# Second attention: quotients in the layout of the value products, causal mask in VectorE's row maximum

## Chip, cores and metric

The kernel runs on one core of a Trainium2 chip (trn2). The metric is the time of the device in microseconds (us). Before the change the median of three runs is 2527.09 us (2526.11 to 2530.27).

## What is computed

A post-norm stack over 4 sequences of 1024 tokens with 256 channels, in float32: an attention of 16 heads with 16 channels (normalised and rotated queries and keys), a gated feed-forward layer, a second causal attention, and a routed layer of 12 experts. The change lies in the second attention, of which the reference says:

```python
scores = jnp.einsum('bhqd,bhkd->bhqk', q, k) * scale
scores = jnp.where(causal[None, None], scores, -jnp.inf)
...
scores = scores + head_scales[None, :, None, None] * geo
attn = jax.nn.softmax(scores, axis=-1)
out = jnp.einsum('bhqk,bkhd->bqhd', attn, v).reshape(B, T, C)
return out @ w_out
```

It has 8 heads of 32 channels. The kernel treats them as 2 groups of 4 heads, so that a group fills 128 partitions.

## The kernel before

**The order of the work.** Up to the experts the order of the instructions on each engine is written out by hand: generators yield one unit of attention at a time, and `weave` puts "pieces" of other layers between the units (a piece is a few matmuls with what empties their bank). A tile is filled and freed in the order in which the code asks for it. The scores, the maxima and most pieces share a ring of six PSUM banks (`ps_s`); the value products have one bank (`ps_av`), and one more bank (`ps_m`) takes the denominators of the second attention or the pieces of the first. A first attention (`first_units`, 64 units) and a second attention of another batch (`second_units`, 36 units) follow each other, four times each.

**The second attention of a batch** (`second_units`, L1103). In the first 12 units only `Maxima1.unit` of group 0 runs; a unit is one tile of 128 queries against up to 512 keys, for four heads. L931 makes the scores. On the diagonal (8 of the 12 units) four more matmuls (L940) add a mask to the last 128 columns: they multiply an identity by the mask in bfloat16, and the product is summed in the same bank. Then VectorE takes the negated row maximum of each head (L942). Next come 12 units in which `Attend1` of group 0 and `Maxima1` of group 1 alternate, and 12 units of `Attend1` of group 1 alone. `split` (L944) and `turn` (L955) bring the maxima into the layout of the keys. `Attend1.scores` (L969) makes the transposed scores, from which ScalarE forms exponentials (L989); GpSimd clears what is above the diagonal (L992). `Attend1.values` (L1004) sums the value products in one bank, and in the other the denominators, in a layout where the heads and channels are partitions and 512 queries are columns.

**The end of a query block** (two blocks in each group, so 4 in a batch, 16 in all). ScalarE copies the two banks out (L1025). Some units later `unload` (L1028) turns both copies on TensorE (8 transposes, L1033) into two banks of the ring; VectorE then takes 16 reciprocals per partition (L1036) and multiplies (L1037) into `oq1`, in which tokens are partitions. For the projection `out_project` turns that back: `turn` (L544, four transposes at L549 and a copy at L552) four times in a batch, and `project` (L554) four times. With the residual, `add_residual` (L515) does six VectorE operations for each piece.

**The end of batch 3.** After its last unit the rows are routed, and dispatched in two halves (`dispatch`, L708), with GpSimd sending them; only then do the experts start (L1388).

**The start.** `project_qk(0, 0, first=True)` squares the projections on GpSimd into `sq` (L229, one buffer, in which `sinT` was loaded), and VectorE sums them (L233); L249 is a reciprocal of 128 columns.

Of the kernel before, what the change touches and what calls it, by code (L numbers as in the profile page):

```python
# [19 lines left out]
P = 128  # L20
# [15 lines left out]
def postln_layers_kernel(ctx: ExitStack, tc: tile.TileContext, a: dict, out: bass.AP):  # L36
# [5 lines left out]

    ident = const.tile([P, P], F32, name="ident")
    make_identity(nc, ident)
    mask_h = const.tile([P, P], BF16, name="mask_h")
    nc.gpsimd.memset(mask_h, 0.0)
    nc.gpsimd.affine_select(
        out=mask_h, in_=mask_h, pattern=[[-1, P]], compare_op=ALU.is_ge, fill=NEG, base=0, channel_multiplier=1
    )
    neg_half = const.tile([P, 1], F32, name="neg_half")  # L50
    nc.gpsimd.memset(neg_half, -0.5)
    ident_h = const.tile([P, P], BF16, name="ident_h")
# [49 lines left out]
    with ExitStack() as main:  # L102
# [42 lines left out]
            nc.sync.dma_start(w0[:, c], a["w0qkv"][c * P : (c + 1) * P, :])  # L145
        cosT = fa.tile([P, TB, D0], F32, tag="tmp", bufs=1, name="cosT")
        nc.scalar.dma_start(cosT, a["cos"].rearrange("(t p) d -> p t d", p=P))
        sinT = fa.tile([P, TB, D0], F32, tag="sq", bufs=1, name="sinT")
        nc.scalar.dma_start(sinT, a["sin"].rearrange("(t p) d -> p t d", p=P))
        gam = act.tile([P, 2, D0], F32, tag="avs", bufs=2, name="gam")  # L150
        nc.scalar.dma_start(gam.rearrange("p s d -> p (s d)"), a["gamma"].partition_broadcast(P))
# [51 lines left out]
        def project_qk(b, pr, first=False):  # L203


            def piece(j, big):
# [19 lines left out]
                part = ss[:, 2 * j : 2 * j + 2].rearrange("p t s h -> p (t s h)")  # L226

                def squares():
                    sq = fa.tile([P, 512], F32, tag="sq", bufs=1, name=f"sq0_{b}_{pr}_{j}")  # L229
                    nc.gpsimd.tensor_tensor(sq, x, x, ALU.mult)  # L230

                    def sums():
                        nc.vector.tensor_reduce(part, sq.rearrange("p (h d) -> p h d", d=D0), AX.X, ALU.add)  # L233

                    return sums
# [135 lines left out]
        class Maxima:  # L371


            def __init__(self, b, g, engines):
# [7 lines left out]
                def rotate(s, u):  # L382
                    eng, to_tok = engines[s], (self.tok, tokk)[s]
                    ts = slice(4 * u, 4 * u + 4)
                    x = xr[:, ts, s, hs, :]
                    y = fa.tile(
                        [P, 4, 4, D0], F32, tag="tmp" if eng is nc.gpsimd else "sq", bufs=1, name=f"y0_{b}_{g}_{s}_{u}"
                    )
# [12 lines left out]
                    eng.tensor_tensor(to_tok[:, ts, :, 0:D0], y, over_heads(bt[s], ts), ALU.add)  # L401
                    yield
# [134 lines left out]
                open_rows.add(key)  # L537
                later(1, root)

        def out_project(b, oqs, w, name):  # L540

            oTs = {}

            def turn(h, c, big):  # L544
                if c == 0:
                    oTs[h] = act.tile([P, 2, 512], F32, tag="hT", bufs=1, name=f"oT{name}_{b}_{h}")
                pt = bank(f"pt{name}_{b}_{h}_{c}", big)
                for i in range(4):
                    nc.tensor.transpose(  # L549
                        pt[:, i * P : (i + 1) * P], oqs[b][:, 4 * h + i, c * P : (c + 1) * P], ident  # L550
                    )
                nc.scalar.copy(oTs[h][:, c, :], pt)  # L552

            def project(j, big):  # L554
                ps = bank(f"pp{name}_{b}_{j}", big)
                for i in range(2):
                    q = slice((2 * j + i) % 4 * P, ((2 * j + i) % 4 + 1) * P)
                    for c in range(2):
                        nc.tensor.matmul(  # L559
                            ps[:, i * 256 : (i + 1) * 256], oTs[j // 2][:, c, q], w[:, c, :], start=c == 0, stop=c == 1  # L560
                        )
                for i in range(2):
                    add_residual(b, 2 * j + i, ps[:, i * 256 : (i + 1) * 256], name)

            out = []
            for h in range(2):
                out += [lambda big, h=h, c=c: turn(h, c, big) for c in range(2)]
                out += [lambda big, j=j: project(j, big) for j in (2 * h, 2 * h + 1)]
            return out

        def turn_x(b, j, name, big):

# [342 lines left out]
        class Maxima1:  # L915
# [7 lines left out]
            def unit(self, i):  # L923
# [5 lines left out]
                for h in range(4):  # L929
                    r = slice(32 * h, 32 * h + 32)  # L930
                    nc.tensor.matmul(  # L931
                        scs[h][:, :n],
                        qT[r, t * P : (t + 1) * P],
                        kT[r, u * 512 : u * 512 + n],
                        start=True,
                        stop=not diag,
                    )
                if diag:
                    for h in range(4):
                        nc.tensor.matmul(scs[h][:, n - P : n], ident_h, mask_h, start=False, stop=True)  # L940
                for h in range(4):
                    nc.vector.tensor_reduce(self.part[:, t, u, h : h + 1], scs[h][:, :n], AX.X, ALU.max, negate=True)  # L942

            def split(self, u):  # L944

# [17 lines left out]
        class Attend1:  # L963


            def __init__(self, m, oq):
                self.m, self.oq, self.b, self.g, self.pes, self.avs = m, oq, m.b, m.g, {}, {}

            def scores(self, i):  # L969
                qb, kt = sc_units[i]  # L970
# [33 lines left out]
            def values(self, i):  # L1004
# [15 lines left out]
                            stop=kt == 4 * qb + 3,  # L1020
                        )
                if kt == 4 * qb + 3:
                    for k in range(2):
                        d = act.tile([P, 512], F32, tag="avs", bufs=2, name=f"avs1_{self.b}_{self.g}_{qb}_{k}")
                        nc.scalar.copy(d, self.av[k])  # L1025
                        self.avs[qb, k] = d

            def unload(self, qb):  # L1028
                pt = [ps_s.tile([P, 512], F32, tag="s", name=f"pto1_{self.b}_{self.g}_{qb}_{k}") for k in range(2)]
                for k in range(2):  # L1030
                    for t in range(4):
                        q = slice(t * P, (t + 1) * P)
                        nc.tensor.transpose(pt[k][:, q], self.avs[qb, k][:, q], ident)  # L1033
                p4 = [t.rearrange("p (t h d) -> p t h d", t=4, h=4) for t in pt]
                rc = act.tile([P, 4, 4], F32, tag="rc", bufs=2, name=f"rc1_{self.b}_{self.g}_{qb}")
                nc.vector.reciprocal(rc, p4[1][:, :, :, 0])  # L1036
                nc.vector.tensor_tensor(  # L1037
                    self.oq[:, 4 * qb : 4 * qb + 4, P * self.g : P * self.g + P].rearrange(
                        "p t (h d) -> p t h d", h=4
                    ),  # L1040
                    p4[0],
                    rc.unsqueeze(3).to_broadcast([P, 4, 4, D1]),
                    ALU.mult,
                )


        groups = {}
        oq0, oq1, ends = {}, {}, {}
        both_pool = (nc.gpsimd, nc.gpsimd)

        def first_units(b):
# [50 lines left out]

        def second_units(b):  # L1103

            oq1[b] = act.tile([P, TB, C], F32, tag="oq", bufs=2, name=f"oq1_{b}")
            now = Maxima1(b, 0)
            for i in range(12):
                now.unit(i)
# [7 lines left out]
            last = None  # L1116
            for g in range(G1):
                nxt = Maxima1(b, g + 1) if g + 1 < G1 else None
                at = Attend1(now, oq1[b])
                for i in range(12):  # L1120
                    at.scores(i)
                    if i > 0:
# [2 lines left out]
                        last.values(11)  # L1125
                    if i == 1:
                        now.turn(1)
                        if last is not None:
                            last.unload(1)
# [8 lines left out]
                    if i == 6:  # L1138
                        at.unload(0)
                    yield  # L1140
                last, now = at, nxt
            last.values(11)
            last.unload(1)

        def weave(units, n, pieces, big, mid=(), at=0, side=(), side_at=0, rate=1):

# [132 lines left out]


        def first_end(b):
            return [lambda big: ends[b](big)] + out_project(b, oq0, w0p, "a0")

        def second_end(b):
            return out_project(b, oq1, w1o, "a1") + route(b)

        cut = 19
        stash = []
# [48 lines left out]
        nc.sync.dma_start(b2.rearrange("p e c -> p (e c)"), a["b2"].partition_broadcast(P))  # L1337
        weave(second_units(2), 36, first_end(3) + ffn0(3), True)
        out2 = second_end(2)
        straight(out2[:8] + project1(3))  # L1340
        out3 = out_project(3, oq1, w1o, "a1")
        st, tu, lo = route(3, True)
        steps2, sums2 = dispatch(2, True)
        weave(second_units(3), 23, out2[8:], True, out3[:4] + st[:2], 30, steps2, 18)
        flush()
        ordered.close()

        for piece in tu[:2] + out3[4:6] + lo[:2] + out3[6:]:
            piece(True)
            tick()  # L1350
        steps, sums = dispatch(3, True, 0)
# [186 lines left out]
```

## Time and profile before

| What | Value |
|---|---|
| median of three runs | 2527.09 us |
| the profiled execution, its own time | 2529.43 us |
| its span, first to last instruction | 2527.6 us |
| busy: TensorE, VectorE, ScalarE, GpSimd | 2364.4, 1364.7, 1024.8, 729.4 us |
| granted TensorE clock, mean | 0.956 |
| first 12 units of a second attention, batch 0 | 757.5 to 793 us from the start of the span |

The profile is of one execution. A group of instructions has a line of the code, an engine, an operation, what it writes and reads, a count, its busy time and the mean duration in ns of one. A float32 matmul shows as two records, a transpose or a bfloat16 matmul as one. The durations of matmuls overlap, so what a run of them costs TensorE is read from the distance between two starts in the timeline. "Idle before" is the time in which the engine had nothing to do before those instructions, with whom it waited for.

### The profile page before, as it was taken

Reading aid. Unit: us, or ns where it says so; the run is one execution under the profiler, and the core shown is the slowest. Engines: PE = TensorE matmul, PEld = TensorE weight load, DVE = VectorE, ACT = ScalarE, POOL = GpSimd, SP = SyncE. Lnnn points to the kernel's source line nnn. Section 1 sums busy time; section 2 is a strip of 40 time slices with the busy share of each in tenths; the row PEclk is TensorE's granted clock in tenths of the full one; section 3 lists DMA queues with packets and bytes.
Section 4 is the critical chain, followed back from the end, with each engine's and each line's share of the span. In section 5 each row is a group of like instructions: output and inputs, shape, how many; then the busy total and the mean of one; then the engine's idle time right before and its main releaser. Section 6 shows DMA issues by size and latency. Waiting matters only on the chain.

```text
span 2527.6 us, 36682 instructions
## 1 busy us (share of the span) xinstructions
PE 2364.4 (94%) x14452; PEld 1194.9 (47%) x14452; DVE 1364.7 (54%) x3157; ACT 1024.8 (41%) x2015; POOL 729.4 (29%) x1015
## 2 busy tenths in 40 slices
PE   6999999999999999999999999999999983999993
PEld 3343334444445543444445434445566442666662
DVE  6765654766657447787563677817435654111112
ACT  1355554545552445545424455461331331111122
POOL 5633623425114122454121320211110143122213
PEclk8999999999998999999989999999998985999996
DMA  3034212000000000001000000112000012444434
GB/s 92 29 119 135 84 59 83 1 27 1 1 1 27 1 1 1 23 26 51 31 1 1 1 1 1 48 33 86 1 1 1 1 51 68 108 111 103 117 72 141
DMA packets 79612, 109.89 MB, mean 43 GB/s; under 512 B 8784, under 2 KB 68432, under 8 KB 77776
## 3 DMA queue, kind: packets, MB, share of 16 engines
q1 hardware_dynamic: 54336, 80.48, 9.8%
q0 software_dynamic: 9984, 14.82, 3.0%
q10 hardware_dynamic: 15120, 12.27, 1.7%
q8 instruction: 113, 1.85, 0.3%
q14 instruction: 59, 0.48, 0.1%
HBM read 68.64 MB, written 38.90 MB: 43 GB/s over the span
## 4 chain that ended last, share of the span: by engine, by line
PE 85%; DVE 8%; DMA 3%; POOL 2%; ACT 1%; issue 1%; SPq 0%; ACTq 0%; DVEq 0%; POOLq 0%
PE sc L458 19%; PE av L476 10%; PE ph L1410 7%; PE py L1426 7%; PE gu L595 7%; PE mx L434 4%; PE sc L978 4%; PE mx L931 4%; PE p L898 4%; PE dn L611 3%; PE av L1015 3%; PE dn L1015 2%; DVE part L942 2%; PE qk L298 2%; PE ppa L559 2%; PE pt L425 2%
## 5 line engine op out<-in xcount | busy, mean ns | idle before, releaser
L437 DVE TENSOR_REDUCE part<-mx 128x1 f32<-128x512 f32 x1024 | 656.5, 685 | 344.3 <-PE mx L434 338.6
L467 ACT ACTIVATE pe<-sc 128x512 f32<-128x512 f32 x1024 | 554.1, 596 | 394.5 <-PE mx L434 341.8
L434 PE MATMUL mx<-kT,qT 32*128 32x512 f32 x2048 | 650.3, 644 | 6.0 <-DVE part L437 5.7
L458 PE MATMUL sc<-qT,kT 32*128 32x512 f32 x2048 | 616.3, 638 | 0.2 <-ACT pe L467 0.2
L458 PEld LDWEIGHTS sc<-qT,kT 32*128 32x128 f32 x2048 | 182.1, 183 | 223.8 <-issue 177.7
L476 PE MATMUL av<-pe,va 128*32 128x512 f32 x2048 | 272.8, 605 | 0.0
L942 DVE TENSOR_REDUCE part<-mx 128x1 f32<-128x512 f32 (+3 forms) x384 | 186.9, 550 | 152.3 <-PE mx L940 108.6
L434 PEld LDWEIGHTS mx<-kT,qT 32*128 32x128 f32 x2048 | 196.6, 185 | 52.7 <-DVE part L437 27.4
L989 ACT ACTIVATE pe<-sc 128x512 f32<-128x512 f32 (+3 forms) x384 | 157.6, 499 | 156.4 <-PE sc L978 156.1
L1410 PE MATMUL ph<-dmT,f 128*128 128x512 f32 x384 | 170.3, 602 | 4.4 <-DVE dmT L90 3.5
L1426 PE MATMUL py<-f,hTm 128*128 128x256 f32 x768 | 167.7, 379 | 0.0
L1418 ACT ACTIVATE hTm<-ph,b 128x512 f32<-128x512 f32 x96 | 60.8, 684 | 261.3 <-PE ph L1410 261.3
L992 POOL TENSOR_SCALAR_AFFINE_SELECT pe<-pe 128x256 f32<-128x256 f32 x128 | 51.7, 411 | 374.6 <-ACT pe L989 372.4
L1426 PEld LDWEIGHTS py<-f,hTm 128*128 128x128 f32 x768 | 145.9, 190 | 25.0 <-issue 5.7
L1430 POOL DMA_INDIRECT acc_d<-yo,dm x48 | 74.5, 1552 | 284.9 <-DVE yo L1428 238.8
L931 PE MATMUL mx<-kT,qT 32*128 32x512 f32 (+3 forms) x768 | 138.6, 593 | 8.5 <-DVE part L942 4.8
L356 POOL TENSOR_TENSOR ss<-ss,neg_half 128x16 f32<-128x16 f32 x48 | 138.7, 2907 | 0.5
L1427 DVE TENSOR_TENSOR yo<-py,b 128x256 f32<-128x256 f32 x48 | 20.4, 425 | 207.6 <-PE py L1426 207.6
L476 PEld LDWEIGHTS av<-pe,va 128*32 128x32 f32 x2048 | 40.3, 108 | 193.9 <-issue 183.9
L978 PE MATMUL sc<-qT,kT 32*128 32x512 f32 (+3 forms) x768 | 117.9, 546 | 1.7 <-DVE part L942 0.6
L1410 PEld LDWEIGHTS ph<-dmT,f 128*128 128x128 f32 x384 | 72.9, 192 | 94.9 <-issue 86.7
L595 PE MATMUL gu<-xTf,wg 128*128 128x256 f32 x384 | 107.7, 403 | 0.0
(357 smaller groups left out, 2938.0 us busy)
## 6 DMA issues: line engine op xcount, KB each, us to landing
f<-in_fc SPq DMA_DIRECT2D x14, 1024.0 KB, 5.0
f<-in_fc ACTq DMA_DIRECT2D x10, 1024.0 KB, 6.0
xink<-in_xT SPq DMA_DIRECT2D x32, 256.0 KB, 2.8
disp_d<-empty SPq DMA_DIRECT2D x12, 520.0 KB, 5.1
qk_d<-xs SPq DMA_DIRECT2D x6, 1024.0 KB, 3.9
xr<-qk_d SPq DMA_DIRECT2D x6, 1024.0 KB, 6.5
dm<-disp_d SPq DMA_DIRECT2D x11, 520.0 KB, 3.7
xinv<-in_xT SPq DMA_DIRECT2D x16, 256.0 KB, 3.1
```

The lines of the kernel that those rows point to most:

```text
L434: nc.tensor.matmul(sc, self.qT[r, t * P : (t + 1) * P], self.kT[r, u * 512 : (u + 1) * 512], start=True, stop=True)
L437: return lambda: nc.vector.tensor_reduce(self.part[:, t, u, h : h + 1], sc, AX.X, ALU.max, negate=True)
L458: nc.tensor.matmul(sc, self.m.kT[r, kt * P : (kt + 1) * P], self.m.qT[r, qb * 512 : (qb + 1) * 512], start=True, stop=True)
L467: nc.scalar.activation(self.pes[i, h // 2][:, h % 2, :], sc, AF.Exp)
L476: nc.tensor.matmul(self.av[32 * h : 32 * h + 32, :], va0[:, kt, 4 * self.g + h, :], self.pes[i, h // 2][:, h % 2, :], start=kt == 0, stop= ...
L595: nc.tensor.matmul(ps[:, i * 256 : (i + 1) * 256], w[:, c, f * P : (f + 1) * P], xT[j][:, c, :], start=c == 0, stop=c == 1,)
L931: nc.tensor.matmul(scs[h][:, :n], qT[r, t * P : (t + 1) * P], kT[r, u * 512 : u * 512 + n], start=True, stop=not diag,)
L942: nc.vector.tensor_reduce(self.part[:, t, u, h : h + 1], scs[h][:, :n], AX.X, ALU.max, negate=True)
L978: nc.tensor.matmul(scs[h][:, off:], ones_h[r, :] if w else kT[r, kt * P : (kt + 1) * P], (self.m.nmT if w else qT)[r, q], start=w == 0, st ...
L989: nc.scalar.activation(pe[:, j, off:], scs[2 * hp + j][:, off:], AF.Exp)
L1410: nc.tensor.matmul(ph[:, i * CAP : (i + 1) * CAP], f1[:, c, (f + i) * P : (f + i + 1) * P], dmT[:, c, :], start=c == 0, stop=c == 1,)
L1426: nc.tensor.matmul(py[:, :C], hT[:, f, c * P : (c + 1) * P], f2[:, f, :], start=f == 0, stop=f == FF1 // P - 1)
```

## The change

- At the end of a query block VectorE takes the reciprocal of the whole bank of denominators (128 x 512) and multiplies it with the bank of value products, in their own layout. The two copies, the eight transposes and `unload` are gone.
- The product is already what the projection needs as its weights, so the second attention's projection has no turns. Its list of pieces is 4 long and not 8, and the slices of these lists are changed to match. Two empty pieces (`wait`) stand behind the two projections in the last `weave`.
- On the diagonal, L940 is gone. VectorE adds a mask of 512 columns (zeros, and the triangle in the last 128) and takes the minimum of the negated sum in one instruction. It writes its sum into `masked`, of which there is one buffer.
- `sinT`, the squares at the start and one temporary go into a buffer ring of two (`q1`) and not into `sq`, which is gone.

```diff
+    mask_w = const.tile([P, 512], BF16, name="mask_w")
+    masked = const.tile([P, 512], BF16, name="masked")
...
-        sinT = fa.tile([P, TB, D0], F32, tag="sq", bufs=1, name="sinT")
+        sinT = act.tile([P, TB, D0], F32, tag="q1", bufs=G1, name="sinT")
...
-                    sq = fa.tile([P, 512], F32, tag="sq", bufs=1, name=f"sq0_{b}_{pr}_{j}")
+                    sq = act.tile([P, 512], F32, tag="q1", bufs=G1, name=f"sq0_{b}_{pr}_{j}")
...
+        def out_project1(b):
+            def project(j, big):
+                project_out(b, j, lambda c, i: oT1[b][:, c, (2 * j + i) * P : (2 * j + i + 1) * P], w1o, "a1", big)
+            return [lambda big, j=j: project(j, big) for j in range(4)]
...
-                        stop=not diag,
+                        stop=True,
                     )
-                if diag:
-                    for h in range(4):
-                        nc.tensor.matmul(scs[h][:, n - P : n], ident_h, mask_h, start=False, stop=True)
                 for h in range(4):
-                    nc.vector.tensor_reduce(self.part[:, t, u, h : h + 1], scs[h][:, :n], AX.X, ALU.max, negate=True)
+                    part = self.part[:, t, u, h : h + 1]
+                    if diag:
+                        nc.vector.tensor_tensor_reduce(
+                            masked[:, :n], scs[h][:, :n], mask_w[:, 512 - n :], -1.0, -NEG, ALU.add, ALU.min, part
+                        )
+                    else:
+                        nc.vector.tensor_reduce(part, scs[h][:, :n], AX.X, ALU.max, negate=True)
...
                 if kt == 4 * qb + 3:
-                    for k in range(2):
-                        d = act.tile([P, 512], F32, tag="avs", bufs=2, name=f"avs1_{self.b}_{self.g}_{qb}_{k}")
-                        nc.scalar.copy(d, self.av[k])
-                        self.avs[qb, k] = d
+                    rc = act.tile([P, 512], F32, tag="avs", bufs=2, name=f"rc1_{self.b}_{self.g}_{qb}")
+                    nc.vector.reciprocal(rc, self.av[1])
+                    nc.vector.tensor_tensor(
+                        self.oT[:, self.g, qb * 512 : (qb + 1) * 512], self.av[0], rc, ALU.mult
+                    )
...
-        straight(out2[:8] + project1(3))
-        out3 = out_project(3, oq1, w1o, "a1")
+        straight(out2[:4] + project1(3))
+        out3 = out_project1(3)
...
-        weave(second_units(3), 23, out2[8:], True, out3[:4] + st[:2], 30, steps2, 18)
+        weave(second_units(3), 23, out2[4:], True, out3[:2] + [wait] * 2 + st[:2], 30, steps2, 18)
...
-        for piece in tu[:2] + out3[4:6] + lo[:2] + out3[6:]:
+        for piece in tu[:2] + lo[:1] + out3[2:3] + lo[1:2] + out3[3:]:
```

More of the change, by code (lines that the diff above doesn't have):

```diff
@@ L44, in postln_layers_kernel @@
     make_identity(nc, ident)
-    mask_h = const.tile([P, P], BF16, name="mask_h")
-    nc.gpsimd.memset(mask_h, 0.0)
+    mask_w = const.tile([P, 512], BF16, name="mask_w")
+    nc.gpsimd.memset(mask_w, 0.0)
     nc.gpsimd.affine_select(
-        out=mask_h, in_=mask_h, pattern=[[-1, P]], compare_op=ALU.is_ge, fill=NEG, base=0, channel_multiplier=1
+        out=mask_w[:, 384:512],
+        in_=mask_w[:, 384:512],
+        pattern=[[-1, P]],
+        compare_op=ALU.is_ge,
+        fill=NEG,
+        base=0,
+        channel_multiplier=1,
     )
+    masked = const.tile([P, 512], BF16, name="masked")
     neg_half = const.tile([P, 1], F32, name="neg_half")
@@ L385, in rotate @@
                     x = xr[:, ts, s, hs, :]
-                    y = fa.tile(
-                        [P, 4, 4, D0], F32, tag="tmp" if eng is nc.gpsimd else "sq", bufs=1, name=f"y0_{b}_{g}_{s}_{u}"
-                    )
+                    if eng is nc.gpsimd:
+                        y = fa.tile([P, 4, 4, D0], F32, tag="tmp", bufs=1, name=f"y0_{b}_{g}_{s}_{u}")
+                    else:
+                        y = act.tile([P, 4, 4, D0], F32, tag="q1", bufs=G1, name=f"y0_{b}_{g}_{s}_{u}")
                     z = fa.tile([P, 4, 4, D0], F32, tag="tmpz", bufs=1, name=f"z0_{b}_{g}_{s}_{u}")
@@ L538, in add_residual, with project_out, out_project0 @@
                 later(1, root)
-        def out_project(b, oqs, w, name):
+        def project_out(b, j, oT, w, name, big):
+            ps = bank(f"pp{name}_{b}_{j}", big)
+            for i in range(2):
+                for c in range(2):
+                    nc.tensor.matmul(
+                        ps[:, i * 256 : (i + 1) * 256], oT(c, i), w[:, c, :], start=c == 0, stop=c == 1
+                    )
+            for i in range(2):
+                add_residual(b, 2 * j + i, ps[:, i * 256 : (i + 1) * 256], name)
+        def out_project0(b):
             oTs = {}
@@ L545, in turn @@
                 if c == 0:
-                    oTs[h] = act.tile([P, 2, 512], F32, tag="hT", bufs=1, name=f"oT{name}_{b}_{h}")
-                pt = bank(f"pt{name}_{b}_{h}_{c}", big)
+                    oTs[h] = act.tile([P, 2, 512], F32, tag="hT", bufs=1, name=f"oTa0_{b}_{h}")
+                pt = bank(f"pta0_{b}_{h}_{c}", big)
                 for i in range(4):
                     nc.tensor.transpose(
-                        pt[:, i * P : (i + 1) * P], oqs[b][:, 4 * h + i, c * P : (c + 1) * P], ident
+                        pt[:, i * P : (i + 1) * P], oq0[b][:, 4 * h + i, c * P : (c + 1) * P], ident
                     )
@@ L554, in project, with oT @@
             def project(j, big):
[L555 to L563, printed above, removed]
+                def oT(c, i):
+                    t = (2 * j + i) % 4
+                    return oTs[j // 2][:, c, t * P : (t + 1) * P]
+                project_out(b, j, oT, w0p, "a0", big)
             out = []
@@ L935, in unit @@
                         start=True,
-                        stop=not diag,
+                        stop=True,
                     )
-                if diag:
-                    for h in range(4):
-                        nc.tensor.matmul(scs[h][:, n - P : n], ident_h, mask_h, start=False, stop=True)
                 for h in range(4):
-                    nc.vector.tensor_reduce(self.part[:, t, u, h : h + 1], scs[h][:, :n], AX.X, ALU.max, negate=True)
+                    part = self.part[:, t, u, h : h + 1]
[3 more added lines that the diff above has]
+                        )
+                    else:
+                        nc.vector.tensor_reduce(part, scs[h][:, :n], AX.X, ALU.max, negate=True)
             def split(self, u):
@@ L963, in postln_layers_kernel, with __init__ @@
         class Attend1:
-            def __init__(self, m, oq):
-                self.m, self.oq, self.b, self.g, self.pes, self.avs = m, oq, m.b, m.g, {}, {}
+            def __init__(self, m, oT):
+                self.m, self.oT, self.b, self.g, self.pes = m, oT, m.b, m.g, {}
             def scores(self, i):
@@ L1022, in values @@
                 if kt == 4 * qb + 3:
-                    for k in range(2):
-                        d = act.tile([P, 512], F32, tag="avs", bufs=2, name=f"avs1_{self.b}_{self.g}_{qb}_{k}")
-                        nc.scalar.copy(d, self.av[k])
-                        self.avs[qb, k] = d
[L1028 to L1044, printed above, removed]
+                    rc = act.tile([P, 512], F32, tag="avs", bufs=2, name=f"rc1_{self.b}_{self.g}_{qb}")
+                    nc.vector.reciprocal(rc, self.av[1])
+                    nc.vector.tensor_tensor(
+                        self.oT[:, self.g, qb * 512 : (qb + 1) * 512], self.av[0], rc, ALU.mult
+                    )
         groups = {}
-        oq0, oq1, ends = {}, {}, {}
+        oq0, oT1, ends = {}, {}, {}
         both_pool = (nc.gpsimd, nc.gpsimd)
@@ L1103, in second_units @@
         def second_units(b):
-            oq1[b] = act.tile([P, TB, C], F32, tag="oq", bufs=2, name=f"oq1_{b}")
+            oT1[b] = act.tile([P, G1, S], F32, tag="oq", bufs=2, name=f"oT1_{b}")
             now = Maxima1(b, 0)
@@ L1118, in second_units @@
                 nxt = Maxima1(b, g + 1) if g + 1 < G1 else None
-                at = Attend1(now, oq1[b])
+                at = Attend1(now, oT1[b])
                 for i in range(12):
@@ L1127, in second_units @@
                         now.turn(1)
-                        if last is not None:
-                            last.unload(1)
                     if nxt is not None:
@@ L1137, in second_units @@
                             nxt.split(1)
-                    if i == 6:
-                        at.unload(0)
                     yield
@@ L1142, in second_units @@
             last.values(11)
-            last.unload(1)
         def weave(units, n, pieces, big, mid=(), at=0, side=(), side_at=0, rate=1):
@@ L1281, in first_end @@
         def first_end(b):
-            return [lambda big: ends[b](big)] + out_project(b, oq0, w0p, "a0")
+            return [lambda big: ends[b](big)] + out_project0(b)
         def second_end(b):
-            return out_project(b, oq1, w1o, "a1") + route(b)
+            return out_project1(b) + route(b)
         cut = 19
```

## The prediction

> **What bounds the kernel now.** I read the page, the chain that ended last, the groups by shape, the busy time by stages, and the timeline around one end of a query block.
>
> ```profile
> PE 85%; DVE 8%; DMA 3%; POOL 2%; ACT 1%; issue 1%; SPq 0%; ACTq 0%; DVEq 0%; POOLq 0%
> ```
>
> TensorE carries 85% of the chain, so a matmul that goes is worth its slot, and work added to VectorE is free where VectorE isn't late. Where is it late? The groups, then the first 12 units of each of the four second attentions:
>
> ```profile
> L942 DVE TENSOR_REDUCE part<-mx 128x1 f32<-128x512 f32 x192 | 119.2, 683 | 53.9 <-PE mx L931 43.4 <-PE mx L940 10.4
> ...
> L1037 DVE TENSOR_TENSOR oq<-pto,rc 128x512 f32<-128x512 f32 x16 | 11.1, 692 | 0.6
> ...
> L1036 DVE RECIPROCAL rc<-pto 128x16 f32<-128x16 f32 x16 | 4.1, 255 | 16.5 <-PE pto L1033 16.5
> ...
> L249 DVE RECIPROCAL ss<-ss 128x128 f32<-128x128 f32 x1 | 1.0, 953 | 0.4 <-ACT ss L248 0.4
> ```
>
> ```profile
> core 0: us, PE busy (x) PEld busy (x) DVE busy (x) ACT busy (x) POOL busy (x), PEclk, DMA share, GB/s
> 757.50:793.00 35.50, 33.93 (x182) 18.62 (x183) 27.74 (x67) 5.20 (x9) 16.78 (x10) 0.86 0.15 47
> 1240.50:1277.00 36.50, 35.08 (x172) 19.72 (x170) 25.95 (x62) 5.48 (x10) 14.73 (x8) 0.77 0.16 53
> 1703.00:1744.00 41.00, 38.48 (x217) 24.91 (x216) 37.63 (x98) 4.48 (x10) 3.73 (x8) 0.96 0.42 149
> 1926.00:1955.00 29.00, 27.38 (x124) 17.06 (x122) 25.27 (x64) 1.27 (x3) 1.86 (x4) 0.70 0.00 1
> ```
>
> VectorE is busy 71 to 92% of these (116.6 of 142 us), and TensorE's weight loads wait for its row maxima in the six-bank ring: VectorE sets the pace there. Once scores and values run too, it doesn't: in the window 829 to 841 VectorE is busy 6.36 of 12 us, TensorE all 12.
>
> ```profile
> 827.95 1.14 PE L931 MATMUL mx<-kT,qT 32*128 32x512 f32 x8
> 829.02 1.09 PE L1033 MATMUL pto<-ident,avs 128*128 128x128 f32 x8
> 829.95 1.03 PE L595 MATMUL gu<-xTf,wg 128*128 128x256 f32 x4
> ```
>
> ```profile
> 815.97 0.39 DVE L520 TENSOR_TENSOR x<-ppa,x 128x256 f32<-128x256 f32 x1
> ...
> 816.96 2.50 DVE L942 TENSOR_REDUCE part<-mx 128x1 f32<-128x512 f32 x4
> 819.38 0.73 DVE L100 TENSOR_SCALAR x<-x,mv_a,rs_a 128x256 f32<-128x256 f32 x2
> ```
>
> The eight turns of an unload take 0.93 us of TensorE (829.02 to 829.95). The second fence is VectorE at the end of a query block (batch 0, whose value products end at 815.3): a residual's six operations, then at once four maxima, then more. There it is late already.
>
> **What goes from TensorE.**
> - Turns of the quotients: 16 unloads at 0.93 us. Four stand at the end of a second attention and are counted with the stalls below; 12 × 0.93 = 11.2 us.
> - Turns before the projection: four transposes take 0.53 us (802.20 to 802.73). 16 pieces; three batches count, batch 3's with its end: 12 × 0.53 = 6.4 us.
> - Mask matmuls: four take 0.23 us (806.50 to 806.73). 64 diagonal units; in the 32 of the first stages VectorE paces, so 32 × 0.23 = 7.4 us.
> - The start: the squares alternate with their sums in one buffer (GpSimd's second square waits 4.49 us for the first sum, at 18.35). With two buffers I replay them from the arrivals of the projections (12.05, 14.28, 16.72, 19.08 us): the last sum ends at 21.2, not 23.9. All after it follows: 2.7 us.
>
> Sum 27.7 us. ScalarE's 48 copies of 0.6 us were off the path: nothing. SP and GpSimd issue the same instructions as before.
>
> **What comes to VectorE: the reciprocal.** It grows from 16 to 512 columns. From 16 (255 ns) and 128 (953 ns) a column costs 6.23 ns, so 953 + 384 × 6.23 = 3345 ns (bounds: 3.2 to 3.6, with PSUM as source, as in the 16-column row). With the product (692 ns) VectorE is blocked for 4.05 us, 16 times, where ScalarE had copied in about 1.2 us. Queued behind it are the next unit's maxima, which free ring banks, and a piece's residual; waiting for it are TensorE's next values, since both accumulator banks are single.
> - Block 0 of group 0: four maxima stand behind it. In batches 0 and 1 the residual stands ahead, so all 4.05 us fall on the maxima (816.96 becomes 821.0), and the scores at 818.07 need banks that these free; with the diagonal's longer maxima before it 4.9 us each. In batch 2 a gate piece (1.9 us) covers part: 2.3. In batch 3 2.8. Sum 14.9.
> - Block 1 of group 0: no maxima, but the next values wait. Batch 0: VectorE ends `split` at 861.7, so quotients at 865.75, and the values that start at 863.10 wait 2.65. Batch 1 the same, batch 2 1.5, batch 3 2.1. Sum 8.9.
> - Block 0 of group 1: a piece and the scores lie between (3.2 us), so 1.1, 1.1, 0.1; in batch 3 there is no piece, and some 3.6 us of dispatch stand ahead of it on VectorE: 6. Sum 8.3.
> - Block 1 of group 1: before, TensorE waited 0.5 us for the copies and turned for 0.93; after, the first attention's maxima wait instead: 0.6 worse twice. In batch 3 the last pieces no longer wait for turns and copies, and GpSimd's sends set the pace anyway: I give back 4 us. Sum -2.8.
>
> Together 29.3 us (bounds: 15, if pieces hide more, and 40).
>
> **What comes to VectorE: the mask.** No row shows this instruction. Nearest is the product of 512 columns with a PSUM source, 692 ns, against 620 from start to start of the maxima (2.48/4). In the changed program's order three of four wait for VectorE's own last instruction, since `masked` is one buffer; the overlap of 65 ns goes. The Trainium skill (VectorE: DVE Perf Modes, section "Two Vector instructions with no wait between them") says that an operation that writes out an accumulator is two instructions, the second a read of it, which no row here shows. By the row alone one costs 0.10 us more than a maximum; by the rule, with a read of 0.075 us (start to start of the smallest operations at 2030.4) to 0.165 (their duration), 0.15 to 0.27. The changed order has these 256 reads; I take 0.22, 56 us of VectorE in all.
> - First stages: 32 units × 4 × 0.22 = 28 us to VectorE's 116.6, makes 145 of 142 us. Some 8 us of its gaps stay (it must wait for the first scores): 10 us longer. Bounds: by the row alone 13 us, which fits the gaps, so 0; at 0.27 and all gaps kept, 23.
> - Other diagonal units: the maximum starts 0.2 us earlier, TensorE's piece hides the rest, except behind a short piece: 3 us (0 to 8).
>
> **The clock.** The Trainium skill (TensorE: Matmul & The Clock Gate, "Why this matters for your kernels") wants no idle gap over some 3 us, else TensorE falls to half clock. The trace is stricter: from 769 to 781 the granted clock was 0.57, with no wait above 1.24 us. Half clock for some 3.4 us (the page's window) loses 1.7 us. By the rule three stalls (4.9, 4.9 and 6 us) qualify, 5.1 us; by the row all eight of 2 us and more might, 14 us. The 6 us one stands at batch 3's end, where GpSimd's sends set the pace, so I take two of the three, 3.5.
>
> **Sum.** -27.7 + 29.3 + 10 + 3 + 3.5 = +18 us on the profiled execution's 2529.4 us (2527.6 of span, 1.8 around it): 2547.5. That execution lay 2.3 us above the median of the runs, so 2545 us.
>
> **The rivals.** About 0.2% (5 us) is what a measurement can tell from no change.
> - VectorE pays more than TensorE gains: the forecast, 2532 to 2570. Against it: VectorE is only 54% busy over all. Chance 0.62.
> - TensorE's slots decide: the pieces between hide the reciprocal (15 us of stalls), the masked maximum fits the gaps (0), and the clock holds: -27.7 + 15 + 1 = -12, 2515 us. For it: 85% of the chain is TensorE. It decides once the fused maximum costs under 0.1 us extra and the stalls average below 1.5 us. Chance 0.14.
> - The two cancel, with a stall of some 1.5 us and 3 us in the first stages: 2522 to 2532. Chance 0.12.
> - The masked maximum streams slower than one column per 1.3 ns, or its read waits the pipeline out: 0.5 us extra gives 64 us to the first stages and drags the mixed units too: 2590. Against it: both two-input rows run at 1.3 to 1.6 ns a column. Chance 0.12.
>
> Faster 0.14, same 0.12, slower 0.74. The range for 8 in 10 is 2518 to 2578: the low end takes in most of the second rival, the high end the upper bounds of two terms together.
>
> **What would show it.** Right: reciprocals near 3.3 us; TensorE waiting for VectorE 2 to 5 us behind them; masked maxima of 0.7 us and reads of 0.1 to 0.2; first stages longer by 2 to 4 us each; mixed units away from block ends shorter by 0.2. Wrong: a reciprocal far from 3.3 us, a fused maximum that costs no more than the old one, or batch 3's end moving by more than a few us, which I know least.

## The result and the profile after

The changed kernel takes 2589.98 us, median of 4 runs (2588.65 to 2594.44); before, 2526.6 (2524.49 to 2530.27). The ratio is 1.0255 (95% interval 1.0239 to 1.0270): slower by 2.55%, outside the predicted range of 2518 to 2578. The profiled execution took 2590.03 us, with a span of 2588.3, 60.7 us more than before.

The chain of waits of the changed kernel:

```profile
PE 82%; DVE 11%; DMA 2%; POOL 2%; issue 1%; ACT 1%; SPq 0%; ACTq 0%; DVEq 0%; POOLq 0%
```

TensorE's share fell from 85 to 82%, VectorE's rose from 8 to 11%. The groups by shape give the new instructions' durations (busy us and mean ns after the bar, then the idle time ahead and what ended it):

```profile
L969 DVE TENSOR_REDUCE part<-mx 128x1 f32<-128x512 f32 x128 | 79.3, 682 | 34.3 <-PE mx L955 34.3
...
L1052 DVE RECIPROCAL rc<-dn 128x512 f32<-128x512 f32 x16 | 53.6, 3347 | 10.5 <-PE dn L1042 10.5
...
L965 DVE CUSTOM_DVE_ANT_0 masked<-mx,mask_w 128x512 bf16<-128x512 f32 x64 | 44.2, 690 | 14.3 <-PE mx L955 6.6 <-DVE part L965 0.5
...
L965 DVE DVE_READ_ACCUMULATOR2_ANT part<- 128x1 f32 x256 | 21.2, 83 | 0.0
```

The reciprocal takes 3347 ns (forecast 3345), the masked maximum 690 with a read of 83. So the single prices were right, and the sum was not. Where are the 60.7 us? Batch 0's four stages, before and after (first maxima, units with maxima, units without, next first attention; PEld is TensorE's loading of weights, PEclk the granted clock):

```profile
core 0: us, PE busy (x) PEld busy (x) DVE busy (x) ACT busy (x) POOL busy (x), PEclk, DMA share, GB/s
758.70:797.50 38.80, 37.09 (x204) 20.91 (x200) 32.01 (x82) 6.74 (x13) 18.63 (x13) 0.87 0.13 43
797.50:857.60 60.10, 60.03 (x498) 28.80 (x498) 32.44 (x77) 21.98 (x54) 15.00 (x21) 0.97 0.01 2
857.60:915.40 57.80, 57.29 (x484) 31.52 (x480) 15.32 (x40) 25.00 (x61) 7.31 (x18) 1.00 0.00 1
915.40:1243.10 327.70, 323.97 (x2032) 138.68 (x2032) 235.05 (x498) 176.63 (x335) 115.20 (x171) 0.99 0.06 20
```

```profile
754.40:797.90 43.50, 41.96 (x168) 25.05 (x164) 34.53 (x118) 6.85 (x13) 19.11 (x13) 0.66 0.13 38
797.90:861.70 63.80, 61.74 (x466) 27.94 (x465) 37.17 (x101) 20.89 (x52) 14.47 (x21) 0.96 0.01 1
861.70:923.90 62.20, 58.29 (x468) 30.50 (x466) 21.64 (x44) 23.19 (x56) 7.35 (x18) 0.97 0.00 1
923.90:1254.20 330.30, 326.23 (x2006) 137.23 (x2006) 239.64 (x498) 173.86 (x329) 115.20 (x171) 0.99 0.06 20
```

Each stage is longer, although TensorE has fewer instructions (466 for 498 in the second), and in three of four the clock is lower. In the second stage TensorE is busy 61.74 us for 60.03: less work, more time. The same cuts through all batches (profiled executions, us; the first maxima end where the first value product starts):

| part of the span | before | after | change |
|---|---|---|---|
| start, to the first maxima of second attention | 758.7 | 754.4 | -4.3 |
| first maxima, 4 batches | 171.7 | 187.1 | +15.4 |
| units of both groups, 4 batches | 467.1 | 503.3 | +36.3 |
| between the second attentions | 664.9 | 677.7 | +12.8 |
| after the last value product | 465.2 | 465.8 | +0.6 |

For the third and fourth row together (1132.0 us before, 1181.1 after) I split TensorE's time in three. The clock records have two values only, full and half. *Idle* is length minus busy time; *clock loss* is half of the busy time within half-clock stretches (an estimate: it takes a matmul to last twice as long there); the rest is *work*.

| us | before | after | change | forecast |
|---|---|---|---|---|
| idle | 18.3 | 46.4 | +28.1 | +32.3 (29.3 and 3) |
| clock loss | 7.9 | 31.4 | +23.5 | +3.5 |
| work | 1105.9 | 1103.2 | -2.7 | -25.0 (11.2, 6.4 and 7.4) |

The idle time came out about as forecast. The clock's loss is nearly seven times the forecast, and of the gain in work only a tenth is there. The timeline at the first block end of batch 0 shows both; first before the change, then after (idle time ahead in brackets; sc are scores, av value products, dn denominators):

```profile
818.07 1.54 PE L978 MATMUL sc<-qT,kT 32*128 32x512 f32 x7
...
820.18 1.06 PE L1015 MATMUL av<-pe,va 128*32 128x512 f32 x8
```

```profile
813.34 1.18 PE L1005 MATMUL sc<-qT,kT 32*128 32x512 f32 x8
...
817.22 3.34 DVE L1052 RECIPROCAL rc<-dn 128x512 f32<-128x512 f32 x1
...
818.33 1.86 PE L1005 MATMUL sc<-qT,kT 32*128 32x512 f32 x4
...
820.60 0.69 DVE L1053 TENSOR_TENSOR oT<-av,rc 128x512 f32<-128x512 f32 x1
821.20 2.48 DVE L969 TENSOR_REDUCE part<-mx 128x1 f32<-128x512 f32 x4
...
821.94 1.29 PE L1005 MATMUL sc<-qT,kT 32*128 32x512 f32 x3 [1.74 <-DVE part L969]
...
824.28 1.94 PE L1042 MATMUL av<-pe,va 128*32 128x512 f32 x8
...
825.98 1.39 PE L1042 MATMUL dn<-pe,ones 128*32 128x512 f32 x8
```

The scores wait for the maxima behind the quotient, as forecast. From the first score to the first value product it takes 5.95 us, before 2.11: 3.84 more. Only 1.74 of it counts as idle. Two heads' scores (4 records) start alone, one after the other, and are busy for 1.86 us, where the eight of four heads together take 1.18 (813.34); so a part of the stop hides in busy time. And the wait of 1.74 us is followed by a half-clock stretch from 823.3 to 826.7, and the eight value products in it take 1.94 us; eight of the same at full clock take 1.06 (at 837.35). At the second block end the single accumulator banks show as forecast, with 2.82 us for 2.65:

```profile
869.61 0.69 DVE L1053 TENSOR_TENSOR oT<-av,rc 128x512 f32<-128x512 f32 x1
...
870.45 1.39 PE L1042 MATMUL av<-pe,va 128*32 128x512 f32 x8 [2.82 <-DVE oT L1053]
```

Half clock follows here too (871.1 to 874.5), and at 929.1 after a wait of 1.29 us. It doesn't follow every stop: the same place in batch 2 has a wait of 2.43 us and full clock behind it.

```profile
1865.12 1.06 PE L1042 MATMUL av<-pe,va 128*32 128x512 f32 x8 [2.43 <-DVE oT L1053]
```

Of the 16 block ends of the changed kernel, 10 are followed by 3.4 or 6.8 us of half clock.

### The profile page after: what moved, and what is told of

Its sections match the earlier page's. It is cut to its first block, busy times and chain, and to the rows that moved or that the text cites. A ratio compares the mean times of both kernels' runs of the same rounds, so it can differ in the third digit from the quotient of the medians.

```text
span 2588.3 us, 36180 instructions
## 1 busy us (share of the span) xinstructions
PE 2393.7 (92%) x14004; PEld 1191.5 (46%) x14004; DVE 1435.3 (55%) x3413; ACT 1001.3 (39%) x1967; POOL 730.7 (28%) x1015
## 4 chain that ended last, share of the span: by engine, by line
PE 82%; DVE 11%; DMA 2%; POOL 2%; issue 1%; ACT 1%; SPq 0%; ACTq 0%; DVEq 0%; POOLq 0%
PE sc L467 18%; PE av L485 9%; PE ph L1416 7%; PE py L1432 6%; PE gu L619 6%; PE mx L443 5%; PE sc L1005 4%; PE mx L955 4%; PE p L922 3%; PE dn L635 3%; PE av L1042 3%; PE dn L1042 2%; PE ppa L554 2%; PE qk L306 2%; DVE rc L1052 2%; DVE masked L965 2%
## 5 line engine op out<-in xcount | busy, mean ns | idle before, releaser
L443 PE MATMUL mx<-kT,qT 32*128 32x512 f32 x2048 | 661.6, 644 | 8.2 <-DVE part L446 7.8
L467 PE MATMUL sc<-qT,kT 32*128 32x512 f32 x2048 | 624.5, 639 | 1.5 <-DVE part L446 1.1
L443 PEld LDWEIGHTS mx<-kT,qT 32*128 32x128 f32 x2048 | 200.0, 185 | 64.0 <-DVE part L446 34.8
L965 DVE CUSTOM_DVE_ANT_0 masked<-mx,mask_w 128x128 bf16<-128x128 f32 (+3 forms) x256 | 125.5, 490 | 127.3 <-PE mx L955 97.6
L955 PE MATMUL mx<-kT,qT 32*128 32x512 f32 (+3 forms) x768 | 156.7, 643 | 9.3 <-DVE part L969 3.5
L1424 ACT ACTIVATE hTm<-ph,b 128x512 f32<-128x512 f32 x96 | 60.7, 683 | 261.2 <-PE ph L1416 261.2
L1005 PE MATMUL sc<-qT,kT 32*128 32x512 f32 (+3 forms) x768 | 139.0, 563 | 7.5 <-DVE part L969 5.2
L955 PEld LDWEIGHTS mx<-kT,qT 32*128 32x128 f32 x768 | 77.1, 218 | 74.7 <-issue 29.8
```

Of the source, the lines that this page charges most:

```text
L443: nc.tensor.matmul(sc, self.qT[r, t * P : (t + 1) * P], self.kT[r, u * 512 : (u + 1) * 512], start=True, stop=True)
L467: nc.tensor.matmul(sc, self.m.kT[r, kt * P : (kt + 1) * P], self.m.qT[r, qb * 512 : (qb + 1) * 512], start=True, stop=True)
L955: nc.tensor.matmul(scs[h][:, :n], qT[r, t * P : (t + 1) * P], kT[r, u * 512 : u * 512 + n], start=True, stop=True,)
L965: nc.vector.tensor_tensor_reduce(masked[:, :n], scs[h][:, :n], mask_w[:, 512 - n :], -1.0, -NEG, ALU.add, ALU.min, part)
L1005: nc.tensor.matmul(scs[h][:, off:], ones_h[r, :] if w else kT[r, kt * P : (kt + 1) * P], (self.m.nmT if w else qT)[r, q], start=w == 0, st ...
```

## The experiments

Theory: the quotients' block ends cost most, by waits and by the half clock that follows them. Rival: the masked maxima cost most. The runs say how much each makes. Medians are us; each ratio is to the kernel before on the same chip, with its 95% interval.

**1. The start alone.** The kernel before with

```
-        sinT = fa.tile([P, TB, D0], F32, tag="sq", bufs=1, name="sinT")
+        sinT = act.tile([P, TB, D0], F32, tag="q1", bufs=G1, name="sinT")
```

and the same for `sq` and for VectorE's `y`.

> The kernel before with the third part of the change alone: sinT, the squares of the start and y of VectorE in the two-buffer ring q1. Forecast: 2.7 us less (2524). The stage table of the changed kernel's trace says 4.3 us less by the second attention of batch 0 (2522 to 2523), and nothing after that. Rival: the gain belongs to the rest of the change and this alone gives 0 to 1 us.

2521.58 (ratio 0.9986, 0.9977 to 0.9995; before 2525.51). The start gives 4 us. It is the reference for the next two.

**2. The quotients alone** (with the ring q1): the mask matmuls and plain maxima are put back in the changed kernel for diagonal units.

```
+                if diag:
+                    for h in range(4):
+                        nc.tensor.matmul(scs[h][:, n - P : n], ident_h, mask_h, start=False, stop=True)
...
-                        nc.vector.tensor_tensor_reduce(
-                            masked[:, :n], scs[h][:, :n], mask_w[:, 512 - n :], -1.0, -NEG, ALU.add, ALU.min, part
-                        )
```

> The changed kernel with the mask put back on TensorE (mask matmuls and plain maxima), so: new quotients, projection without turns, ring q1. My own terms: -11.2 - 6.4 - 4.3 (start as measured) + 29.3 + 3.5 (clock) = +11, so 2538 us. Theory 'quotients': the block ends cost more than I gave them, because the maxima behind the reciprocal restart slowly at half clock, and they make most of the 63 us: 2560 to 2575. Theory 'mask': the masked maxima make most of it: 2525 to 2540.

2569.36 (1.0176, 1.0159 to 1.0193), 47.8 us over run 1. The quotients are three quarters of the loss. In the account above, against run 1: idle +27.7, clock loss +20.2, work -4.1 us.

**3. The mask alone** (with q1): the kernel before with the edit of run 2 the other way round.

> The kernel before with the ring q1 and the mask added by VectorE, unloading and projection as before. My own terms: -7.4 + 10 + 3 - 4.3 = +1, so 2528 us. Theory 'mask': first stages longer by 3 to 5 us each with the clock at half through them, mixed units longer too, so 2550 to 2565. Theory 'quotients': 2525 to 2535.

2536.98 (1.0052, 1.0035 to 1.0069), 15.4 over run 1, between the two theories' figures. First maxima 168.2 to 186.4 us (+18.2); the other units and the stages between, 1132.1 to 1133.5, although 32 units there lost their mask matmuls. With runs 1 and 2 the sum is 2584.8; 5 us are left for the two together.

**4. The mask in place.** The changed kernel, without the buffer `masked`:

```
                         nc.vector.tensor_tensor_reduce(
-                            masked[:, :n], scs[h][:, :n], mask_w[:, 512 - n :], -1.0, -NEG, ALU.add, ALU.min, part
+                            scs[h][:, :n], scs[h][:, :n], mask_w[:, 512 - n :], -1.0, -NEG, ALU.add, ALU.min, part
```

> The changed kernel, but the masked scores go back to their own PSUM bank instead of the one buffer masked, so that no masked maximum waits for the one before it. In the trace of the changed kernel 512 columns take 0.84 us from start to start: 0.69 and a read of 0.083, of which 0.075 overlap, and 0.15 of gap. Theory 'wait': the gap is the wait on VectorE's own semaphore; without it 0.69 from start to start, the first stages lose 12 to 20 us in all, 2565 to 2575. Theory 'read': the read of the sum itself holds VectorE, start to start stays at 0.8 and the time at 2585 to 2590.

2566.9 (1.0159, 1.0142 to 1.0176): 23 us less than the changed kernel, 2.5 less than run 2. VectorE's timeline in the changed kernel, then in this one:

```profile
763.09 0.69 DVE L965 CUSTOM_DVE_ANT_0 masked<-mx,mask_w 128x512 bf16<-128x512 f32 x1
763.70 0.08 DVE L965 DVE_READ_ACCUMULATOR2_ANT part<- 128x1 f32 x1
763.93 0.69 DVE L965 CUSTOM_DVE_ANT_0 masked<-mx,mask_w 128x512 bf16<-128x512 f32 x1
```

```profile
757.28 0.73 DVE L964 CUSTOM_DVE_ANT_0 mx<-mx,mask_w 128x512 f32<-128x512 f32 x1
757.93 0.14 DVE L964 DVE_READ_ACCUMULATOR2_ANT part<- 128x1 f32 x1
757.93 0.73 DVE L964 CUSTOM_DVE_ANT_0 mx<-mx,mask_w 128x512 f32<-128x512 f32 x1
```

From start to start it was 0.84 us and is 0.65; a plain maximum has 0.62. Now the next one starts with the read of the one before. In the changed kernel's trace VectorE waits for a semaphore of its own in front of each of these; here that wait is gone. The first maxima fall from 187.1 to 168.9 us, and run 1, with mask matmuls, has 168.2: nearly the whole price of the mask there was this wait, which one shared output buffer made. (The output also moved from SBUF in bfloat16 to PSUM in float32; a second buffer in SBUF wasn't tried.)

**5. Zero matmuls.** The changed kernel with matmuls of a zero tile where the mask matmuls stood, VectorE still adding the mask.

```
+                if diag:
+                    for h in range(4):
+                        nc.tensor.matmul(scs[h][:, n - P : n], ident_h, zero_h, start=False, stop=True)
```

> The changed kernel with the 256 mask matmuls back, but adding zeros; VectorE still adds the mask. In the changed kernel TensorE ran 204.8 us at half clock up to the last value product (before: 112.6), 97.8 of them in the four first stages (before: 59). Theory 'clock sets the first stages': with TensorE busier there, the half clock falls back towards 59 us and the first stages lose 10 us or more, 2575 to 2582. Theory 'VectorE sets them': their length stays within 2 us whatever the clock does, the mixed units pay up to 7 us, 2588 to 2597.

2591.73 (1.0258, 1.0241 to 1.0275). In batch 0's first maxima the half clock fell from 29.3 to 17.9 us and the length from 43.5 to 42.5; in batch 3 from 39.6 to 33.0, and the length stayed at 45.0. All four together had 187.1 us and have 186.7: there VectorE sets the time, not the clock.

**6 and 7. How long is VectorE held?** Run 2 with a copy for the reciprocal (the division is left out), and with a reciprocal of half of the columns (half is left out).

```
-                    nc.vector.reciprocal(rc, self.av[1])
+                    nc.vector.tensor_copy(rc, self.av[1])
```

```
-                    nc.vector.reciprocal(rc, self.av[1])
+                    nc.vector.reciprocal(rc[:, :256], self.av[1][:, :256])
+                    nc.vector.tensor_copy(rc[:, 256:], self.av[1][:, 256:])
```

> As the run with the new quotients alone, but the sums are copied where it forms their reciprocals; this leaves the division out (the routing that follows sees other data). VectorE is held for 1.4 us instead of 4.05 at each block end, the instructions of all other engines are the same. Theory 'the block ends, by wait and by clock': TensorE's idle time falls by some 25 us and the clock's loss by some 30, so 2569 becomes 2512 to 2522. Theory 'waits alone, the clock loss comes from fewer matmuls': 2569 - 25 = 2544, half clock still near 160 us. Theory 'it is the shorter list of pieces': above 2555.

> Between the two: reciprocal of the first 256 columns, a copy of the other 256 (half of the division is left out). VectorE is held for 953 + 128 x 6.23 = 1.75, 0.42 and 0.69, 2.86 us in all. If waits and clock loss both follow the held time in proportion: 2569 - 57 x 1.19/2.67 = 2544. If a short stop costs as many half-clock stretches as a long one: 2569 - 27 x 0.45 = 2557. If the pieces between hide 2.9 us at most block ends: 2530 or less.

6: 2521.82 (0.9984, 0.9977 to 0.9991). 7: 2551.53 (1.0097, 1.0074 to 1.0120). The part after the last value product is as long in run 6 as in run 2 (466.0 and 466.1 us), so the other data show no effect there. The account, for the units and the stages between:

| us | run 1 | run 6 | run 7 | run 2 |
|---|---|---|---|---|
| VectorE held at a block end | - | 1.4 | 2.9 | 4.05 |
| idle | 18.3 | 21.1 | 31.5 | 46.0 |
| half clock | 15.6 | 21.1 | 62.5 | 61.7 |
| clock loss | 7.8 | 10.3 | 30.3 | 28.0 |

The idle time grows with the held time. The half clock doesn't: a stop of 2.9 us brings as much as one of 4.05, one of 1.4 little. In run 7 waits of TensorE of 1.16 and 1.85 us stand ahead of half-clock stretches (from 814.7 and 862.5). So the clock's loss belongs to the stops, and in these executions, one of each, it looks like a step and not a slope. It scatters: run 4 has the block ends of the changed kernel and 37.3 us of clock loss for 31.4.

**8. Sliced quotients.** Run 2, but ScalarE copies the two banks out as before, and VectorE forms the quotients from the copies in two parts, at the next two units.

```
-                    nc.vector.reciprocal(rc, self.av[1])
...
+                        nc.scalar.copy(d[k], self.av[k])
+                    def part(k):
+                        for j in (2 * k, 2 * k + 1):
+                            c = slice(j * P, (j + 1) * P)
+                            nc.vector.reciprocal(d[1][:, c], d[1][:, c])
+                        c = slice(k * 256, (k + 1) * 256)
...
+                        nc.vector.tensor_tensor(self.oT[:, self.g, q], d[0][:, c], d[1][:, c], ALU.mult)
+                    later(1, lambda: part(0))
+                    later(2, lambda: part(1))
```

> As the run with the new quotients alone, but ScalarE copies numerators and sums out at the block's end, as before, and VectorE forms the quotients from these copies in two parts, behind the next two units' maxima (two reciprocals of 128 columns and one product of 256, some 2.3 us each). The work is all there, VectorE's total is the same. Theory 'the block ends': the banks are free after 1.2 us, no wait of TensorE's is over 1 us, the clock stays as before, and the turns that went show as a gain: 2521.6 - 9 to -17, so 2505 to 2513. Theory 'VectorE's total decides' (4.05 us, 16 times): within 10 us of 2569.

2522.81 (0.9992, 0.9983 to 1.0001): 46.5 us of the 47.8 are gone, with the same total on VectorE (busy 1417.9 us, in run 2 1415.8). I had expected 10 to 18 more. Slices and a later place were changed together, and the banks come free earlier; run 11 tells the banks apart. Up to the end of batch 2's second attention it is 7 us ahead of run 1, then loses 1.7 in front of batch 3 and 6.4 in batch 3's last units. That points at the change's other edit, pieces that moved.

**9. Old places.** Run 8, with empty pieces where the turns had stood, so that all other pieces stand as before:

```
-            return [lambda big, j=j: project(j, big) for j in range(4)]
+            p = [lambda big, j=j: project(j, big) for j in range(4)]
+            return [wait] * 2 + p[:2] + [wait] * 2 + p[2:]
```

The slices of `out2`, `out3` and the tail's list are those of before.

> The sliced quotients with mask on TensorE (2522.8), and every other piece back at the place that it had before: empty pieces stand where the turns stood. The change had moved batch 3's first two projections two units forward, next to the dispatch of batch 2. Theory 'moved pieces': of the 6.4 us that sliced quotients lost in group 1 of batch 3, and the 1.7 ahead of batch 3, most come back: 2513 to 2517. Rival, 'the dispatch holds VectorE wherever the projections stand': 2520 to 2524.

2516.4 (0.9958, 0.9944 to 0.9972). Work is 1088.8 us against 1106.0 in run 1: 17.2 less. The turns' gain is real once nothing eats it. Of it 13 go into idle (+9.1) and clock loss (+4.0), so some 5 us show in the time. The timeline of VectorE behind batch 0's first block end:

```profile
814.21 2.50 DVE L960 TENSOR_REDUCE part<-mx 128x1 f32<-128x512 f32 x4
816.63 0.73 DVE L101 TENSOR_SCALAR x<-x,mv_a,rs_a 128x256 f32<-128x256 f32 x2
817.27 1.76 DVE L1050 RECIPROCAL avs<-avs 128x128 f32<-128x128 f32 x2
819.06 0.43 DVE L1053 TENSOR_TENSOR oT<-avs,avs 128x256 f32<-128x256 f32 x1
819.99 0.88 DVE L960 TENSOR_REDUCE part<-mx 128x1 f32<-128x128 f32 x4 [0.50 <-PE mx L958]
```

The maxima come first, the half quotient follows in the gap. And the windows of the two stages of units:

```profile
795.10:854.10 59.00, 58.92 (x490) 28.09 (x490) 35.68 (x81) 21.81 (x54) 13.93 (x21) 0.98 0.00 1
854.10:910.20 56.10, 55.62 (x472) 29.92 (x468) 21.70 (x48) 24.96 (x61) 7.31 (x18) 1.00 0.01 1
```

59.0 and 56.1 us, before 60.1 and 57.8, changed 63.8 and 62.2.

**10. The best version.** Run 9 with the mask in place (run 4's edit).

> The same with the mask added by VectorE in place. With the changed quotients, in place was 2.5 us faster than mask matmuls. The 256 mask matmuls cost TensorE 0.23 us a unit; in the 32 units woven with scores they stand on the path: 7.4 us at most, of which the maximum's 0.03 us (0.65 against 0.62 from start to start) takes little. Theory 'slots': 3 to 6 us under the run with mask matmuls, 2507 to 2513. Theory 'the clock': fewer matmuls bring more half clock, no gain: 2514 to 2520.

2514.45 (0.9955, 0.9941 to 0.9968): 11 us (0.45%) under the kernel before, with an interval clear of 1, and in the range of 'the clock'. Against run 9 the difference of 2 us lies within the scatter of the runs. In the account work is 2.3 us less than in run 9, idle 0.6 and clock loss 3.6 more; the first maxima are 3.6 shorter.

**11. Banks or queue?** Run 2 with the copies of run 8, but the quotients in one piece at once:

```
-                    nc.vector.reciprocal(rc, self.av[1])
...
+                        nc.scalar.copy(d[k], self.av[k])
+                    nc.vector.reciprocal(d[1], d[1])
...
+                        self.oT[:, self.g, qb * 512 : (qb + 1) * 512], d[0], d[1], ALU.mult
```

> As the run with the new quotients alone, but ScalarE copies numerators and sums out first and VectorE then forms the quotients from the copies at once, in one piece. VectorE's queue is held as long as there (4.05 us, 1.2 us later), the two banks are free after 1.2 us. By my split of the waits, 14.9 us for the maxima behind the reciprocal, 8.9 for the banks: the banks' part goes, with its share of half clock: 2569 - 9 - 8, 2548 to 2556. Theory 'maxima alone': above 2562. Theory 'banks alone': 2520 to 2530.

2567.44 (1.0164, 1.0147 to 1.0181), 2 us under run 2, in the range of 'maxima alone': a miss for my split. The units without maxima did gain by free banks (batch 0: 61.6 to 57.3 us, batch 1 the same), but others lost as much (batch 2's units with maxima 66.9 to 71.8), since VectorE is held as long and a little later. Early banks alone are worth nothing clear of the scatter while the queue stays blocked.

**12. Old places, quotients whole.** Run 2 with the edit of run 9.

> The run with the new quotients alone with the other pieces at their old places (empty pieces where the turns stood). Theory 'moved pieces matter beside the stalls': some 5 us less than 2569, at batch 3's end. Theory 'stalls alone': within 3 us of 2569.

2558.86 (1.0132, 1.0117 to 1.0148): 10.5 us less than run 2, twice what I expected. The profiled gain lies mostly in these: the first attention of batch 3 (ahead of batch 2's second) 4.8, batch 2's first maxima 1.2, the pieces in front of batch 3 1.8, batch 3's last units 2.0, its dispatch 1.8. Why moved pieces cost so much in the first attention isn't settled; the runs show only where.

## Why the prediction was wrong

The direction was right; the size was under a third of the true one (+18 for +63). Two terms of the sum failed, by some 20 us each: the clock (3.5 us became 23.5) and what goes from TensorE (25.0 us in the units and the stages between became 2.7).

- **Durations.** Right: reciprocal 3347 ns for 3345; the masked maximum 0.84 us for 0.62 + 0.22.
- **Waits behind the reciprocal, 29.3 us.** About right in sum (+28.1 idle in the change, +27.7 in run 2), in part by luck: of the 4.9 us at block 0 of group 0, 3.84 came in batch 0, and only 1.74 of them as idle time. Wrong in the split: run 11 shows that banks and maxima aren't added; when one is freed, the other stands in its place.
- **The clock, 3.5 us. This step failed.** It measured 23.5 (20.2 in run 2). I let half clock follow two of the three long stalls only, by the skill's 3 us, although I had written that the trace was stricter. Waits of 1.2 to 1.9 us were followed by it as well (the changed kernel and run 7), so 10 of the 16 block ends had 3.4 or 6.8 us of half clock. The bound of 14 us that stood there for all eight stalls of 2 us and more was too low as well, for shorter waits count. No length of one wait decides, for one of 2.43 us brought none; what does is open.
- **What goes from TensorE, 25.0 us (turns 17.6, mask matmuls 7.4). This step failed too.** I took a matmul that goes to be worth its slot, and had read the shortened lists as nothing but fewer turns. The matmuls went, but others, nearly the same in number, became busy for longer. Their busy time in us, with half-clock time counted at half:

| matmuls of | run 1 | run 2 | run 12 | run 8 | run 9 | run 3 | changed |
|---|---|---|---|---|---|---|---|
| scores, units of the second attention | 115.9 | 120.8 | 120.9 | 115.4 | 115.5 | 123.6 | 127.4 |
| maxima and mask, same units | 55.2 | 55.3 | 55.3 | 55.3 | 55.3 | 47.0 | 47.1 |
| maxima, first attentions of batches 2 and 3 | 294.3 | 302.9 | 297.9 | 302.0 | 295.9 | 294.3 | 302.7 |

- **The turns.** Run 9 finds 17.2 us of work gone; run 2 only 4.1. Of the 13 between, 6.3 come back when the other pieces return to their places (run 12), and 6.8 when the stops go as well (run 9). The table shows where: the scores are some 5 us longer with the stops (runs 2 and 12) and not without (8 and 9), and the first attentions' maxima some 8 us longer with moved pieces (2 and 8), 2 to 4 with old places (9 and 12). Why moved pieces lengthen the latter isn't settled. That 17.2 meets the forecast 17.6 is luck in part: I counted 12 unloads and 12 turns, and these stages hold 15 and 14, 21.4 us by their slots.
- **The other mask matmuls.** Their slots went (8.2 us in run 3), but the scores took 7.7 us more; these units and stages are 1.4 us longer there, not shorter. In run 10 idle and clock take back what is left.
- **The first maxima, 10 us.** 15.4 measured (18.2 in run 3), for the 28 us more that I gave VectorE: less of it went into the gaps than I thought. My upper bound of 23 doesn't follow from its terms: at 0.27 us for each of 128 maxima, with all gaps kept, it is 35. The cause of the 0.22 was named in the prediction (the one buffer), but I blamed the read with it; run 4 shows the wait to be nearly all of the price.
- **The start, 2.7 us.** 4 (run 1).
- **Rivals.** "TensorE's slots decide" is near what runs 9 and 10 are, with the stops removed: 2516 and 2514, where I had worked out 2515. That the figures meet is luck: run 9 keeps the mask matmuls, and its terms are others. The fourth case hit 2590 by chance: its mechanism, 0.5 us extra for a masked maximum, isn't there.

So: of the 63 us, the mask alone made 15 (a wait for itself), the quotients 48, the start gave 4 back, and some 5 come of mask and quotients together. The 48 are the stops of VectorE's queue, 42.5 (from run 9 to 12), and the moved pieces, 10.5 (from run 12 to 2), less 5 that the turns give (from run 1 to 9). TensorE's account has 28 us of idle time and 20 of clock loss for the whole of run 2. What part of the clock's loss would stay if TensorE were kept busy through the stops wasn't tried.

## What to carry over

Price a long instruction by what stands behind it in its engine's queue, and add for the stops of the matmul engine the half clock that may follow: here 20 us on 28 of waits. A matmul that goes isn't always worth its slot: look whether others become busy for longer. Cut the long instruction up and put the parts behind the urgent work: here the total work was the same, and the time 46 us less. When pieces leave a list that is spread over units, keep the places of the others, and don't let instructions that follow each other at once share one scratch output.

## What the runs showed of the hardware

- Half clock followed waits of TensorE of 1.16, 1.29, 1.74, 1.85 and 2.82 us, and didn't follow one of 2.43. The Trainium skill (TensorE: Matmul & The Clock Gate, "Why this matters for your kernels") warns of idle gaps over some 3 us; here shorter ones went ahead of half clock, and no length of one gap tells whether it comes.
- A reciprocal of 512 columns takes 3347 ns, nearly five times a product of the same size (692). Two of 128 take 1.76 us.
- Scores of two heads that start one pair after the other are busy for 1.86 us; those of four heads together for 1.18. So busy time of TensorE can grow while its instructions become fewer.
- A maximum of 512 columns with a second operand and an output written in place costs 0.65 us from start to start (run 4), a plain one 0.62. With a wait of VectorE for its own last instruction it is 0.84 (the changed kernel).
